# An attention block's softmax maxima: folded by ScalarE's shift, turned as four blocks one step later

## The chip, the cores and the metric

The kernel runs on one core of one Trainium2 chip. The metric is the device time of one execution in microseconds (us); the time before is 3637.75 us, the median of three runs (3636.31 to 3641.64). The engines are called PE (TensorE's matmuls; PEld its weight loads), ACT (ScalarE), DVE (VectorE), POOL (GpSimd) and SP (the engine that issues most DMAs). PE writes to the accumulation memory PSUM, of which this kernel uses all eight banks in the attention stage; ACT and DVE read it.

## What is computed

The reference is one block of a transformer with modulated layer norms, on x of shape 8 x 1024 x 256: attention with 16 heads of 64, then a mixture of 8 experts of which each takes its 512 best tokens. All of it is float32. Cut to what matters here:

```
h = layernorm(x) * (1 + ca) + sa
proj = einsum('bpv,havn->bhapn', h, w_qkv)         # q, k, v of 16 heads, N = 64
scores = einsum('bhqn,bhkn->bhqk', q, k) / 8
attn = softmax(scores, axis=-1)                    # needs each query's maximum over 1024 keys
out = einsum('bhqk,bhkn->bhqn', attn, v)
x = x + ga * (concat of out @ w_o)
h = layernorm(x) * (1 + cb) + sb                   # then the router, and the experts
```

The change touches the softmax's maxima, the order of the attention loop, and the places where rows of tokens are turned into columns.

## The kernel before

**Units and steps.** Attention is cut into NSU = 128 units: a batch b, a pair p of heads (j = 0, 1), and a half h of the queries (512 of them, QB). Keys lie on the partitions: key tile c (0 to 7) of a unit gives scores `s` of 128 keys x (2 heads x 512 queries). The loop `while g < 4 * NSU + LAG or steps` (L702) goes through steps g; `u, gm = divmod(g, 4)`, so a unit's scores take four steps (gm = 0 to 3 below "step 0" to "step 3"), two key tiles each. The exponentials of key tile c are taken five steps after its scores, the products with the values six steps after (LAG = 6).

**The order is written out by hand** (`tc.manual_schedule()`, L692): each engine runs its instructions in the order in which the program issues them, and an instruction waits for the data and buffers that it needs. Tasks that don't belong to one unit are hung on steps with `at(g, where, f, ...)` and run by `run(g, where)` in the places "load", "m1", "post", "pool" and "m2" of a step.

**A step before**, in order: "load"; in step 1 `max_spread` of the unit before (L705); the subtractions of the maxima from two older key tiles (`subtract`, L415, DVE; in step 3 the second of them comes after the scores); scores of two new key tiles (`scores_mm` L356 on PE, then `scores_out`: ACT copies them to `p`, L365, and DVE updates the running maximum `top`, L370); "m1" (projections); "post"; the exponentials (`exp_of`, L418, ACT); the values of two older tiles (`values_mm`, L427, PE), after the last of a unit `values_out` (copy `oT`, L436, ACT); `add_up` (L438 to L446, POOL: sums of the exponentials); in step 3 `max_turn` and `split_max`; "pool"; "m2".

**The maxima.** After eight key tiles `top` (128 x 2 x 512) holds for each query the maximum over 8 keys, for 128 key positions. `max_turn` (L372) turns it on PE as eight 128x128 blocks into `tt`; `split_max` (L381) reduces `tt` along the free axis on DVE, negated, and splits each maximum into three bfloat16 parts in four small operations. `max_rows` (L395, step 0 of the next unit, "m1") turns the parts to rows `pn`, which ACT copies to `nr` (L404). `max_spread` (L407) multiplies them with ones, which leaves the negated maximum of every query on all partitions in `less`. `subtract` adds `less` to the kept scores.

**Buffers in PSUM.** `ps_s` has two buffers of two banks for the scores (tag "s"), which `tt` uses too. `ps_b` has one (two banks) for `less`, `ps_av` one bank for `av`, and `ps_m` one bank, tag "mm". This single `mm` buffer is taken in turn by the projections `pq` (L321) and `pv` (L338), `pn` (L399), `pd` (L462), the output projection `po` (L537), the turned rows `ptx` (L295) and `pth` (L574) and the router's product `pl` (L589). The next user waits until the last one has been read.

**Other tasks of the attention loop.** `qk_task` and `v_task` project queries, keys and values of the coming pair: three projections a unit, one in each of steps 1, 2 and 3. `den_out` (L451, step 0, "m2") sums the exponentials over the keys into `pd`; ACT copies it to `den` (L470), and `den_load`, `den_inv`, `den_spread`, `den_mul` bring the reciprocals back through DRAM and scale `oT`, which is stored to DRAM. `ln_task` normalises 256 rows of a coming batch and turns them (`ln_out`, L286). `out_proj`, `out_norm`, `out_turn`, `out_route`, `out_exp`, `out_score`, `out_store` finish the batch before: output projection, residual, second norm, router. `free_slot` gives `ln_out`, `out_proj` and `out_turn` a step 3 ("behind" the turn of the maxima), and `out_route` a step 1 or 2.

Turns of rows, before, are products with the identity over two halves of 64 columns:

```
for m in range(2):
    c0 = k * P + m * N
    nc.tensor.matmul(pt[m * N : (m + 1) * N, k, i * P : (i + 1) * P],
                     xt[:, i, c0 : c0 + N], ident, start=True, stop=True)
```

Of the kernel before, what the change touches and what calls it, by code (L numbers as in the profile page):

```python
# [37 lines left out]
P = 128  # L38
# [4 lines left out]
def adaln_block(  # L43
# [178 lines left out]
    def mod_rows(i):  # L222
# [13 lines left out]
        for i in (0, 3):  # L236
# [3 lines left out]
            size = small.tile([B, D], F32, tag="at", name=f"size{i}", bufs=2)  # L240
# [45 lines left out]
    def ln_out(b, t):  # L286
        if t == 0:
            hTs[b] = work.tile([P, KC, S], F32, tag="hT", name=f"hT{b}")
        xt = ln_x.pop((b, t))[0]
        pt = ps_m.tile([P, KC, 2 * P], F32, tag="mm", name=f"ptx{b}_{t}")  # L290
        for k in range(KC):
            for i in range(2):
                for m in range(2):
                    c0 = k * P + m * N
                    nc.tensor.matmul(  # L295
                        pt[m * N : (m + 1) * N, k, i * P : (i + 1) * P],
                        xt[:, i, c0 : c0 + N], ident, start=True, stop=True,
                    )
        for k in range(KC):
            nc.vector.tensor_scalar(  # L300
                hTs[b][:, k, 2 * t * P : (2 * t + 2) * P], pt[:, k, :],
                modT[:, KC + k, b : b + 1], modT[:, k, b : b + 1],
                op0=ALU.mult, op1=ALU.add,
            )
# [66 lines left out]

    def max_turn(u):  # L372
        top = tops.pop(u)
        turned[u] = ps_s.tile([P, 8, P], F32, tag="s", name=f"tt{u}")
        for j in range(2):
            for t in range(4):
                nc.tensor.transpose(  # L377
                    turned[u][:, 4 * j + t, :], top[:, j, t * P : (t + 1) * P], ident
                )

    def split_max(u):  # L381

        tt = turned.pop(u)
        nm = tt[:, :2, :8]
        nc.vector.tensor_reduce(nm[:, 0, :], tt, AX.X, ALU.max, negate=True)  # L385
        part = [
            parts_of[u % 2][:, :, :, i].rearrange("p t j -> p j t") for i in range(3)
        ]
        whole, rest = (nm[:, i, :].rearrange("p (j t) -> p j t", j=2) for i in range(2))
# [5 lines left out]
    def max_rows(u):  # L395
# [7 lines left out]
        rows_of[u] = work.tile([P, QB], BF16, tag="nr", name=f"nr{u}")  # L403
# [139 lines left out]
    def out_add(b, t, po):  # L543
        n = f"{b}_{t}"
        x1 = o_x[b, t]
        tmp = small.tile([P, D], F32, tag="at", name=f"at{n}", bufs=2)
# [18 lines left out]
    def out_turn(pool, b, t, tag="mm"):  # L565
# [3 lines left out]
        for i in range(2):  # L569
            h2 = o_h[b, t + i]  # L570
            for k in range(KC):
                for m in range(2):
                    c0 = k * P + m * N
                    nc.tensor.matmul(  # L574
                        pt[m * N : (m + 1) * N, i, k, :], h2[:, c0 : c0 + N], ident,
                        start=True, stop=True,
                    )
# [60 lines left out]
    taken = set()  # L638

    def free_slot(g, behind=False):  # L640
        while g in taken or g % 4 == 0 or behind != (g % 4 == 3):
            g += 1
        taken.add(g)
        return g

    for t in range(NT // 2):
        at(-15 + t, "m2", ln_out, 0, t)
        ln_task(1, t, free_slot(39 + 4 * t, True))
    for b in range(B):
        for p in range(NP):  # L650
            P0 = 8 * (b * NP + p)
            for i, g in enumerate((-7, -6, -5, -2)):
                at(P0 + g, "m1", qk_task, b, p, i)
            if p % 2 == 0:
                for t, g in enumerate((-9, -3, -1, 5)):
# [4 lines left out]
            at(P0 + 17, "load", den_load, b, p)  # L660
            at(P0 + 18, "post", den_inv, b, p)
            at(P0 + 19, "load", den_spread, b, p)
            at(P0 + 20, "pool", den_mul, b, p)
        if b + 1 < B:
            if b + 2 < B:
                for t in range(NT // 2):
                    ln_task(b + 2, t, free_slot(64 * (b + 1) + 39 + 4 * t, True))
            for t in range(NT):
                g = free_slot(64 * (b + 1) + 19 + 4 * t, True)
# [3 lines left out]
                if t % 2:  # L673
                    g = free_slot(g + 2, True)
                    at(g, "m2", out_turn, ps_m, b, t - 1)
                    g = free_slot(g + 1)
                    at(g, "m2", out_route, ps_m, b, t - 1)
                    at(g + 1, "post", out_exp, b, t - 1)
                    at(g + 2, "post", out_score, b, t - 1)
                    at(g + 3, "pool", out_store, b, t - 1)  # L680
    for u in range(NSU):
        at(4 * u + 4, "m1", max_rows, u)
        if u < NSU - 1:
            at(4 * u + 12, "m2", den_out, u)
# [6 lines left out]

    with tc.manual_schedule():  # L692
# [9 lines left out]
        while g < 4 * NSU + LAG or steps:  # L702
            u, gm = divmod(g, 4)
            run(g, "load")
            if gm == 1 and 0 < u <= NSU:  # L705
                max_spread(u - 1)
            u1, gm1 = divmod(g - LAG + 1, 4)
            late = [(u1, 2 * gm1 + i) for i in range(2) if 0 <= u1 < NSU]

            for uc in late[: 1 if gm == 3 else 2]:  # L710
                subtract(*uc)
            if 0 <= u < NSU:
                for c in (2 * gm, 2 * gm + 1):
                    scores_out(u, c, scores_mm(u, c))
            if gm == 3 and late:
                subtract(*late[1])
            run(g, "m1")
            run(g, "post")
            for uc in late:
                exp_of(*uc)  # L720
            u1, gm1 = divmod(g - LAG, 4)
            if 0 <= u1 < NSU:
                for c in (2 * gm1, 2 * gm1 + 1):
                    values_mm(u1, c)
                    if u1 == NSU - 1:
                        if c == 0:
# [354 lines left out]
```

## Time and profile before

| | |
|---|---|
| median of 3 runs | 3637.75 us |
| the profiled execution | 3636.69 us, span 3635.0 us |
| granted PE clock over the span | 0.983 |
| attention loop, first to last `less` product | 82.3 to 3214.8 us |
| PE busy in it | 3095.78 of 3132.50 us |
| DVE, ACT, POOL busy in it | 2674.07, 2354.09, 2533.91 us |
| after the loop: last output projections, search, experts | some 420 us |

Profiles are of one execution. A row of the timeline gives the start, the length, the engine, the line, the operation, what it writes and reads with their shapes, how many instructions were merged into it, and in brackets how long the engine was idle before it and what ended that. PE's ends are modelled, so PE work is best read from start to start. Busy time is summed for each engine; the last rows of some of the costliest groups around the change:

```
L356 PE MATMUL s<-qk,qk 64*128 64x512 f32 x4096 | 1024.9, 612 | 36.1 <-DVE parts L393 32.3
L370 DVE TENSOR_TENSOR top<-top,s 128x1024 f32<-128x1024 f32 x768 | 936.9, 1220 | 259.9 <-ACT p L365 218.2
L385 DVE TENSOR_REDUCE tt<-tt 128x8 f32<-128x1024 f32 x128 | 157.4, 1230 | 67.7 <-PE tt L377 67.6
L377 PE MATMUL tt<-ident,top 128*128 128x128 f32 x1024 | 139.9, 280 | 3.1 <-DVE top L370 3.1
```

The columns are line, engine, operation, output and inputs, shapes and count; then busy us and mean ns of one; then the idle time of the engine just ahead of them and what ended most of it.

### The profile page before, as it was taken

How to read it: one execution, taken by the hardware profiler on the slowest of the kernel's cores; microseconds unless marked ns; L12 is line 12 of the kernel's file. 1: busy time of each engine (PE TensorE's matmuls, PEld its weight loads, DVE VectorE, ACT ScalarE, POOL GpSimd, SP SyncE). 2: the span in 40 equal slices, each digit the busy share in tenths (PEclk: the TensorE clock that was granted, in tenths of full speed). 3: DMA queues.
4: the chain of work that ended last, by engine and by line, in shares of the span. 5: the costliest groups of instructions: out<-in, count | busy, mean ns of one | idle time of the engine just before them, and what ended most of it. 6: DMA issues, size and time to landing. Idle time of an engine off the chain costs nothing. (4 is left out here: it accounts for less than half of the span.)

```text
span 3635.0 us, 54304 instructions
## 1 busy us (share of the span) xinstructions
PE 3462.8 (95%) x20670; PEld 1460.7 (40%) x20670; DVE 2904.0 (80%) x3651; ACT 2432.8 (67%) x2980; POOL 2657.6 (73%) x1537
## 2 busy tenths in 40 slices
PE   6999999999999999999999999999999999982898
PEld 2333334334433434334433344344334344342565
DVE  4888888888888888888888888888888888857442
ACT  2777777777777777777777777777777777740111
POOL 0778778887788777977788888877888887851232
PEclk9999999999999999999999999999999999995999
DMA  3010011111121122111211112011311112133332
GB/s 76 13 38 29 24 31 57 45 43 41 49 56 38 45 61 55 33 39 45 65 52 30 52 45 62 30 52 43 62 38 43 46 51 56 51 85 122 94 99 41
DMA packets 189653, 185.40 MB, mean 51 GB/s; under 512 B 48952, under 2 KB 167240, under 8 KB 189264
## 3 DMA queue, kind: packets, MB, share of 16 engines
q1 hardware_dynamic: 170736, 160.04, 15.6%
q0 software_dynamic: 7168, 12.72, 1.8%
q10 hardware_dynamic: 11488, 9.18, 0.9%
q8 instruction: 163, 2.67, 0.3%
q14 instruction: 98, 0.80, 0.1%
HBM read 127.06 MB, written 63.21 MB: 52 GB/s over the span
## 5 line engine op out<-in xcount | busy, mean ns | idle before, releaser
L446 POOL TENSOR_TENSOR acc<-acc,p 128x1024 f32<-128x1024 f32 x762 | 1805.2, 2369 | 361.8 <-ACT p L418 328.5
L365 ACT COPY p<-s 128x1024 f32<-128x1024 f32 x1024 | 996.2, 1018 | 421.1 <-PE s L356 414.5
L415 DVE TENSOR_TENSOR p<-p,less 128x1024 f32<-128x1024 f32 x1024 | 1206.7, 1210 | 32.8 <-PE less L412 30.0
L370 DVE TENSOR_TENSOR top<-top,s 128x1024 f32<-128x1024 f32 x768 | 936.9, 1220 | 259.9 <-ACT p L365 218.2
L418 ACT ACTIVATE p<-p 128x1024 f32<-128x1024 f32 x1024 | 1041.7, 1057 | 75.0 <-DVE p L415 74.7
L356 PE MATMUL s<-qk,qk 64*128 64x512 f32 x4096 | 1024.9, 612 | 36.1 <-DVE parts L393 32.3
L427 PE MATMUL av<-p,v 128*64 128x512 f32 x4096 | 968.1, 593 | 1.8 <-ACT oT L436 1.8
L356 PEld LDWEIGHTS s<-qk,qk 64*128 64x128 f32 x4096 | 358.3, 186 | 528.7 <-issue 240.1
L321 PE MATMUL pq<-hT,wq 128*64 128x512 f32 x2048 | 495.9, 605 | 2.7 <-ACT qk L328 1.4
L427 PEld LDWEIGHTS av<-p,v 128*64 128x64 f32 x4096 | 280.6, 137 | 461.9 <-issue 367.3
L443 POOL TENSOR_TENSOR acc<-p,p 128x1024 f32<-128x1024 f32 x127 | 301.6, 2375 | 190.4 <-ACT p L418 190.4
L321 PEld LDWEIGHTS pq<-hT,wq 128*64 128x64 f32 x2048 | 124.1, 136 | 343.0 <-issue 211.4
L338 PE MATMUL pv<-wq,hT 128*64 128x256 f32 x2048 | 251.0, 387 | 2.6 <-ACT qk L326 1.4
L1006 ACT ACTIVATE h<-ph,b_sb 128x512 f32<-128x512 f32 x64 | 44.0, 687 | 274.6 <-PE ph L1002 274.6
L385 DVE TENSOR_REDUCE tt<-tt 128x8 f32<-128x1024 f32 x128 | 157.4, 1230 | 67.7 <-PE tt L377 67.6
L537 PE MATMUL po<-wo,ot 128*64 128x256 f32 x1792 | 205.7, 382 | 0.0
L338 PEld LDWEIGHTS pv<-wq,hT 128*64 128x64 f32 x2048 | 136.4, 137 | 155.5 <-issue 66.2
L370 DVE TENSOR_TENSOR top<-p,s 128x1024 f32<-128x1024 f32 x128 | 155.9, 1218 | 9.8 <-ACT p L365 9.8
L343 ACT COPY v<-pv 128x512 f32<-128x512 f32 x128 | 74.9, 585 | 129.7 <-PE pv L338 129.7
L377 PEld LDWEIGHTS tt<-ident,top 128*128 128x128 f32 x1024 | 109.6, 140 | 107.2 <-DVE top L370 107.2
L508 POOL TENSOR_TENSOR oT<-oT,rb 128x1024 f32<-128x1024 f32 x63 | 149.9, 2380 | 3.3 <-DMA rb<-rden_d 3.3
L537 PEld LDWEIGHTS po<-wo,ot 128*64 128x64 f32 x1792 | 123.5, 137 | 66.2 <-issue 9.4
(166 smaller groups left out, 2429.7 us busy)
## 6 DMA issues: line engine op xcount, KB each, us to landing
rb<-rden_d SPq DMA_DIRECT2D x128, 256.0 KB
oT_d<-oT SPq DMA_DIRECT2D x62, 512.0 KB
ot<-oT_d SPq DMA_DIRECT2D x56, 512.0 KB
rows_d<-row SPq DMA_DIRECT2D x64, 132.0 KB
rows_d<-gb_d SPq DMA_DIRECT2D x8, 1024.0 KB
w<-in_L_ffn_w_dram ACTq DMA_DIRECT2D x8, 1024.0 KB
w<-in_L_ffn_w_dram SPq DMA_DIRECT2D x8, 1024.0 KB
lnx<-in_L_attn_inputs_dram SPq DMA_DIRECT2D x28, 256.0 KB
```

The lines of the kernel that those rows point to most:

```text
L321: nc.tensor.matmul(pq[m * N : (m + 1) * N, :], wq_of(k, a, 2 * p + m), hTs[b][:, k, sl], start=(k == 0), stop=(k == KC - 1),)
L338: nc.tensor.matmul(pv[m * N : (m + 1) * N, i, :], hTs[b][:, k, t0 : t0 + N], wq_of(k, 2, 4 * g, 4), start=(k == 0), stop=(k == KC - 1),)
L356: nc.tensor.matmul(ps[:, j, :], kt[r, c * P : (c + 1) * P], qt[r, h * QB : (h + 1) * QB], start=True, stop=True,)
L365: nc.scalar.copy(probs[u, c], ps)
L370: nc.vector.tensor_tensor(tops[u], probs[u, 0] if c == 1 else tops[u], ps, ALU.max)
L385: nc.vector.tensor_reduce(nm[:, 0, :], tt, AX.X, ALU.max, negate=True)
L415: nc.vector.tensor_tensor(probs[u, c], probs[u, c], less[u], ALU.add)
L418: nc.scalar.activation(probs[u, c], probs[u, c], AF.Exp)
L427: nc.tensor.matmul(avs[u][j * N : (j + 1) * N, :], v[:, c, hh * N : (hh + 1) * N], pT[:, j, :], start=(c == 0), stop=(c == NT - 1),)
L443: nc.gpsimd.tensor_tensor(sums[u], pts[0], pts[1], ALU.add)
L446: nc.gpsimd.tensor_tensor(sums[u], sums[u], pt, ALU.add)
L537: nc.tensor.matmul(po[m * N : (m + 1) * N, :], ot[:, p, m * N : (m + 1) * N], wo[:, p, :], start=(p == 0), stop=(p == NP - 1),)
```

## The change

**The maxima.** A new `max_shift` at the end of step 3 copies, on ACT, each head's opposite half of the partitions of `top` into a tile in the `mm` buffer, moved by 64 partitions: two copies of 64 x 512. A new `max_halves` at the start of step 0 of the next unit takes, on DVE, the maximum of the two halves, head 0 on partitions 0 to 63 and head 1 on 64 to 127: two maxima of 64 x 512. `max_turn` then turns four 128x128 blocks instead of eight, and `split_max` reduces 512 elements a partition instead of 1024.

**The order.** The turn moves from the end of step 3 into step 0 of the next unit, behind that unit's first scores and the older values, which run ahead of it there. `max_rows` moves from "m1" of step 0 to the end of step 0. `max_spread` stays in step 1 but comes after the new scores, and in step 1 both subtractions come after `max_spread`. `den_out` moves one step, to step 1. Projections stand in steps 0, 2 and 3.

**Turns of rows** in `ln_out` and `out_turn` become PE transposes of whole 128x128 blocks; `ln_out`'s scaled copy to `hT` moves from DVE to ACT. `ln_task` now works on the next batch, in its first units, instead of the one after; output projections, `ln_out` and `out_turn` stand in step 2, `out_route` in a new place "m3" of step 1.

In the diff `turning` is `gm == 0 and 0 < u <= NSU`, `late` and `new` are the key tiles to be subtracted and scored in the step, and `values()` issues the products with the values of the two older ones. The diff (the buffer counts of `size`, `nr` and `at`, and that of the last tile's sum, are left out):

```diff
@@ ln_out
-                for m in range(2):
-                    c0 = k * P + m * N
-                    nc.tensor.matmul(
-                        pt[m * N : (m + 1) * N, k, i * P : (i + 1) * P],
-                        xt[:, i, c0 : c0 + N], ident, start=True, stop=True,
-                    )
+                nc.tensor.transpose(
+                    pt[:, k, i * P : (i + 1) * P], xt[:, i, k * P : (k + 1) * P], ident
+                )
         for k in range(KC):
-            nc.vector.tensor_scalar(
-                hTs[b][:, k, 2 * t * P : (2 * t + 2) * P], pt[:, k, :],
-                modT[:, KC + k, b : b + 1], modT[:, k, b : b + 1],
-                op0=ALU.mult, op1=ALU.add,
+            nc.scalar.activation(
+                hTs[b][:, k, 2 * t * P : (2 * t + 2) * P], pt[:, k, :], AF.Identity,
+                bias=modT[:, k, b : b + 1], scale=modT[:, KC + k, b : b + 1],
             )
@@
+    shifted = {}
+    def max_shift(u):
+        shifted[u] = ps_m.tile([P, QB], F32, tag="mm", name=f"shift{u}")
+        for j in range(2):
+            nc.scalar.copy(
+                shifted[u][j * N : (j + 1) * N, :], tops[u][(1 - j) * N : (2 - j) * N, j, :]
+            )
+    def max_halves(u):
+        top, other = tops.pop(u), shifted.pop(u)
+        tops[u] = work.tile([P, QB], F32, tag="half", name=f"half{u}", bufs=1)
+        for j in range(2):
+            r = slice(j * N, (j + 1) * N)
+            nc.vector.tensor_tensor(tops[u][r, :], top[r, j, :], other[r, :], ALU.max)
     def max_turn(u):
         top = tops.pop(u)
-        turned[u] = ps_s.tile([P, 8, P], F32, tag="s", name=f"tt{u}")
-        for j in range(2):
-            for t in range(4):
-                nc.tensor.transpose(
-                    turned[u][:, 4 * j + t, :], top[:, j, t * P : (t + 1) * P], ident
-                )
+        turned[u] = ps_s.tile([P, 2, QB], F32, tag="s", name=f"tt{u}")
+        for t in range(4):
+            sl = slice(t * P, (t + 1) * P)
+            nc.tensor.transpose(turned[u][:, 0, sl], top[:, sl], ident)
     def split_max(u):
-        nm = tt[:, :2, :8]
-        nc.vector.tensor_reduce(nm[:, 0, :], tt, AX.X, ALU.max, negate=True)
+        nm = tt[:, 1, :16].rearrange("p (i t j) -> p i t j", i=2, j=2)
+        nc.vector.tensor_reduce(
+            whole, tt[:, 0, :].rearrange("p (t j k) -> p t j k", t=4, j=2), AX.X, ALU.max,
+            negate=True,
+        )
@@ out_turn
-                for m in range(2):
-                    c0 = k * P + m * N
-                    nc.tensor.matmul(
-                        pt[m * N : (m + 1) * N, i, k, :], h2[:, c0 : c0 + N], ident,
-                        start=True, stop=True,
-                    )
+                nc.tensor.transpose(pt[:, i, k, :], h2[:, k * P : (k + 1) * P], ident)
@@ the tasks' steps
-            for i, g in enumerate((-7, -6, -5, -2)):
+            for i, g in enumerate((-8, -6, -5, -2)):
                 at(P0 + g, "m1", qk_task, b, p, i)
-                for t, g in enumerate((-9, -3, -1, 5)):
+                for t, g in enumerate((-9, -4, -1, 4)):
                     at(P0 + g, "m1", v_task, b, p // 2, t)
-            at(P0 + 17, "load", den_load, b, p)
+            at(P0 + 18, "load", den_load, b, p)
...
-                    ln_task(b + 2, t, free_slot(64 * (b + 1) + 39 + 4 * t, True))
+                ln_task(b + 1, t, 64 * b + 2 + 4 * t)
-                g = free_slot(64 * (b + 1) + 19 + 4 * t, True)
+                g = 64 * (b + 1) + 18 + 4 * (t + t // 2)
                 at(g - 2, "load", out_load, b, t)
                 at(g, "m2", out_proj, ps_m, b, t)
                 at(g + 1, "pool", out_norm, b, t)
...
+                    at(g + 4, "m2", out_turn, ps_m, b, t - 1)
+                    at(g + 7, "m3", out_route, ps_m, b, t - 1)
+                    at(g + 8, "post", out_exp, b, t - 1)
+                    at(g + 9, "post", out_score, b, t - 1)
+                    at(g + 10, "pool", out_store, b, t - 1)
     for u in range(NSU):
-        at(4 * u + 4, "m1", max_rows, u)
         if u < NSU - 1:
-            at(4 * u + 12, "m2", den_out, u)
+            at(4 * u + 13, "m2", den_out, u)
@@ the step
             run(g, "load")
-            if gm == 1 and 0 < u <= NSU:
-                max_spread(u - 1)
-            for uc in late[: 1 if gm == 3 else 2]:
+            early = (1, 0, 2, 1)[gm]
+            for uc in late[:early]:
                 subtract(*uc)
-            if 0 <= u < NSU:
-                for c in (2 * gm, 2 * gm + 1):
-                    scores_out(u, c, scores_mm(u, c))
-            if gm == 3 and late:
-                subtract(*late[1])
+            if turning:
+                max_halves(u - 1)
+            for uc in new:
+                scores_out(*uc, scores_mm(*uc))
+            if gm == 1 and 0 < u <= NSU:
+                max_spread(u - 1)
+            if turning:
+                values()
+                max_turn(u - 1)
+                split_max(u - 1)
+            for uc in late[early:]:
+                if gm != 3:
+                    subtract(*uc)
             run(g, "m1")
             run(g, "post")
-            for uc in late:
+            for uc in late[: 1 if gm == 3 else 2]:
                 exp_of(*uc)
+            if gm == 3:
+                if new:
+                    max_shift(u)
+                for uc in late[early:]:
+                    subtract(*uc)
+                    exp_of(*uc)
+            if not turning:
+                values()
...
-            if gm == 3 and 0 <= u < NSU:
-                max_turn(u)
-                split_max(u)
             run(g, "pool")
             run(g, "m2")
+            run(g, "m3")
+            if turning:
+                max_rows(u - 1)
```

## The prediction

> **What bounds the kernel now.** First the page's engine shares and its clock row.
>
> ```profile
> PE 3462.8 (95%) x20670; PEld 1460.7 (40%) x20670; DVE 2904.0 (80%) x3651; ACT 2432.8 (67%) x2980; POOL 2657.6 (73%) x1537
> PEclk9999999999999999999999999999999999995999
> ```
>
> Then the totals of the attention stretch alone, from the first `less` product (82.3 us) to the last (3214.8 us): 127 units in 3132.5 us, 24.67 us a unit, PE busy 3095.8 us of it. Idle PE is worth 37 us in all, so PE work sets the time. Then the timeline of one unit, in which PE rows follow each other without gaps:
>
> ```profile
> 1504.53 1.95 PE L338 MATMUL pv<-wq,hT 128*64 128x256 f32 x16
> ...
> 1506.31 1.89 PE L427 MATMUL av<-p,v 128*64 128x512 f32 x8
> 1506.52 0.59 ACT L343 COPY v<-pv 128x512 f32<-128x512 f32 x1 [0.74 <-PE pv L338]
> ...
> 1507.00 2.00 ACT L418 ACTIVATE p<-p 128x1024 f32<-128x1024 f32 x2
> ...
> 1508.12 1.99 PE L356 MATMUL s<-qk,qk 64*128 64x512 f32 x8
> ...
> 1508.91 0.57 ACT L436 COPY oT<-av 128x512 f32<-128x512 f32 x1
> ...
> 1519.14 1.09 PE L377 MATMUL tt<-ident,top 128*128 128x128 f32 x8
> ...
> 1520.16 1.09 PE L295 MATMUL ptx<-ident,lnx 128*64 128x128 f32 x16
> ```
>
> From start to start: pv to av 1.78 us, av to s 1.81, s to the next row (pq at 1510.04) 1.92, eight turns 1.02, ptx 1.02. A second thing to see: a projection that ends on PE is copied out by ACT 1.99 us after it started (1504.53 to 1506.52), and rows of one engine in a chain overlap by about 0.1 us (1506.52 + 0.59 against 1507.00).
>
> Last, waits that show what the single buffers do:
>
> ```profile
> 42.38 1.94 PE L321 MATMUL pq<-hT,wq 128*64 128x512 f32 x8 [0.69 <-ACT qk L328]
> ...
> 3219.28 1.15 PE L427 MATMUL av<-p,v 128*64 128x512 f32 x4 [1.80 <-ACT oT L436]
> ```
>
> and from the list of waits (us in total, times, longest):
>
> ```profile
> DVE top L370 <- ACT p L365: 228.0, 238, 2.4
> ```
>
> A projection can't start before the last user of the one `mm` buffer has been copied out; `av` can't before `oT` has; and the running maximum of a key tile waits for ACT's copy of the same scores.
>
> **The change, part by part** (steps 0 to 3 of a unit; c0 to c7 are its key tiles; PE sums are start to start).
>
> Saved on PE: four turns instead of eight. Half of 1.02 is 0.51; with a change of array shape on top (scores cost 1.92 after another shape, 1.81 after `less`, so 0.11) 0.62; I take 0.55, 0.47 saved in 128 units: 60 us. The turns of `ptx` and `pth` on the whole array are four such turns in place of 1.02 us: 0.47 x 56 in the stretch = 26 us. Idle PE at the turn: up to 37 us. One more change of shape (turns, then a projection): -0.11 x 127 = -14 us. Together 109 us: this is what PE work alone promises.
>
> Added off PE: two shifts of 64x512 on ACT. No such row; the nearest are 0.57 (`oT`, 512 columns) and 1.01 (scores, 1024). I take 0.58 each, bounds 0.4 and 1.0. Two maxima of 64x512 on DVE: between 0.43 (L547, 256 columns) and 1.22 (1024), 0.69 each; the reduction halves from 1.23 to 0.70. DVE's total grows by 128 x (1.38 - 0.53) less 30 us of `hT`, about 80 us on 2674; ACT's by 128 x 1.1 and the `hT` writes on 2354. Neither reaches PE. The `hT` writes on ACT come last in step 2, behind its exponentials, and the next scores are copied later; I cost them at nothing, and without that cover at 28 x 1 us.
>
> Moved: this decides. In step 1 the diff puts the scores c2, c3 ahead of `max_spread`, and both subtractions (c0, c1 of the unit before) behind the maxima of c2, c3 on DVE. `den_out` moves from step 0 to step 1. No projection is left in step 1; there is one each in steps 0, 2 and 3. Each engine runs its queue in order, so I follow one unit from the start of its step-0 projection on PE:
>
> - ACT copies that projection out at +1.99 (row: 0.58, then 2.00 for the two exponentials queued behind it, then 0.59 for `nr`, which `max_rows` now issues last in step 0). With 0.1 overlaps, `nr` ends at +4.98.
> - Behind `nr` on ACT stands the copy of c2, start +4.88, 1.01 long. DVE's maximum of c2 waits for it. The maxima of c2, c3 take 2.54 (row pair), the two subtractions 2.35 with 0.08 overlap: the second ends at +10.75.
> - ACT's exponential of c1 waits for that: 1.06, then `oT` 0.57, then `den` 0.37 (the copy of `pd`), 0.2 of overlap: +12.58, and 0.1 until PE sees it.
> - `pd` holds the one `mm` buffer. The step-2 projection waits for it on PE, and everything behind it.
>
> That is 12.66 us from the step-0 projection to the step-2 projection. PE's own work between them is projection 1.78, `pn` 0.25, scores 1.92, `less` 0.23, values 1.82, `pd` 0.57, scores 1.92: 8.49. So PE stands 4.2 us: about 0.9 ahead of `pn` (its buffer waits for the projection's copy), 0.3 ahead of `less` (for `nr`), 3.0 ahead of the step-2 projection. From there to the next step-0 projection PE runs through: 1.78 + 1.82 + 1.92 + 1.78 + 1.82 + 1.92 + 1.82 + 0.55 = 13.4. **A unit takes 26.1 us before extra work, the stall included.** The shift isn't on this loop: from the last maximum over two shifts, an exponential, two score copies, c1's maximum, reduction, four small splits and a subtraction I reach the last exponential within 0.1 us of when ACT is free. At 1.0 us a shift it would add 0.8 a unit, 100 us.
>
> Extra work on top, all in PE's running part: 56 output projections of 3.60 (L537 row of 32, start to start) = 202; 56 turns of 0.55 = 31. The 28 router products now stand behind `pd` in step 1 and take its wait, so the next scores (1.92) and they (0.52) come after it: 2.45 x 28 = 69. The 28 score normalisations (L611 to L615, 1.9 us on DVE) now stand between the maximum and the last subtraction in step 3 and use up 0.9 us of cover ahead of the turns: 1.0 x 28 = 28. Stretch: 127 x 26.1 + 202 + 31 + 69 + 28 = 3645, against 3132.5: +512. On the profiled execution (3636.7, its span 3635.0, 1 us under the median of 3637.75): 4148.
>
> What the stall does to the clock is the other term. The trace has one lone stall of that kind:
>
> ```profile
> 3213.40:3216.80 3.40, 3.40 (x24) 0.90 (x22) 2.44 (x3) 2.46 (x4) 3.32 (x2) 1.00 0.00 0
> 3216.80:3220.20 3.40, 1.60 (x22) 0.69 (x18) 3.37 (x6) 3.33 (x6) 3.32 (x2) 0.99 0.03 4
> 3220.20:3223.60 3.40, 3.40 (x18) 0.70 (x20) 3.33 (x9) 3.33 (x4) 0.48 (x3) 0.51 0.06 16
> ...
> 62.90:66.30 3.40, 2.00 (x10) 0.59 (x10) 2.90 (x4) 1.56 (x3) 0.00 (x0) 1.00 0.06 10
> 66.30:69.70 3.40, 3.40 (x18) 1.07 (x16) 1.22 (x1) 2.07 (x4) 0.00 (x0) 1.00 0.00 0
> ```
>
> The columns are the stretch, its length, busy PE, PEld, DVE, ACT and POOL, then the granted clock. After 3.4 us with PE busy 1.60 the clock was 0.51 for the next 3.4; after 2.00 busy it stayed. A 3.0 us hole leaves under 1.6 busy in some 3.4 us piece for about nine positions in ten. A half-clock piece costs 1.7 us where it falls on work; some falls on the rest of the hole. I take 1.4 us a unit (bounds 0 and 1.7), on PE's running part: 127 x 1.4 = 178. **4148 + 178 = 4326, and I predict 4325.**
>
> The Trainium skill, TensorE: Matmul & The Clock Gate, section "What's actually happening", asks for a wholly idle window of about 3.4 us before the clock halves. By that rule a 3.0 us hole costs nothing more and the time would be 4148; the row, with a window half busy, speaks against it, and the row decides.
>
> Moved without a price: normalisation of the next batch into steps early in the current one (its `mm` buffer is free after the projection's copy); the denominators' DMAs on SP one step later as a chain, `den` waiting for its copy, with a step (6 us) and more to the next issue; the first output load only three steps behind the store it reads, about 18 us for 512 KB; POOL's sums, 4.8 us a step of over 6. If the load came late, a few us in seven batches.
>
> **The rivals.**
> 1. PE work alone counts: DVE and ACT keep up, and the step-2 projection finds its buffer free. 3637 - 109 = **3528**. For it: PE is 95% busy, the saved rows are real. Against it: the queue orders above. The point from which it decides: subtractions that end less than 5 us after ACT's copy of c2. 10%.
> 2. The loop as above at full clock: **4148**. For it: the rule of the clock isn't known from one event. 22%.
> 3. The maximum's own chain is the longer loop (shift near 1.0, or handing over partitions slower than a copy) with half clock: **4430** and more. The two shifts have no row. 8%.
> 4. Stall and savings cancel: needs a stall of 0.9 us a unit, which no order of these rows gives. 2%.
>
> **Numbers.** The forecast has 58%, own range 4250 to 4430. With rival 2 it makes 80%: 4080 to 4450. Below about 0.2% this kernel's times can't be told apart. Faster 0.10, the same 0.02, slower 0.88.
>
> **What would show it.** Right: PE idle ahead of a projection (L321) released by ACT `den` L470, near 3 us, in nearly every unit; `less` products about 26 us apart where no output projection lies between; subtraction rows of c0, c1 behind two maxima; PEclk tenths below 9 all along. Turns: four rows of L377's kind, near 0.55 a unit. Wrong: PE rows without gaps at step 2, or a granted clock of 1.00 beside 3 us holes (then 4148).

## The result, and the profile after

The changed kernel takes 4445.6 us (median of four runs, 4443.4 to 4449.3) against 3639.7 for the kernel before beside it: **1.222 times** as long, interval 1.220 to 1.224. That is 808 us more than the time the prediction started from, and inside its range at the upper edge (4450). The profiled execution has a span of 4447.5 us.

The page of the changed kernel, its engine shares and its clock row:

```profile
PE 3715.4 (84%) x19390; PEld 1467.5 (33%) x19390; DVE 3018.3 (68%) x3843; ACT 2607.0 (59%) x3300; POOL 2654.7 (60%) x1537
PEclk9999999899998999989999899989999899897699
```

PE was busy 95% of the span; now 84%, of a longer span, although it has 1280 instructions fewer. Its busy time has grown by 253 us with less work in it: the same products took longer, because the granted clock (mean 0.919, 0.983 before) fell again and again. No other engine has taken over: DVE, ACT and POOL all show lower shares than before. When all shares fall, look at waits.

The list of waits of the changed kernel (us in total, times, longest):

```profile
PE pq L317 <- ACT den L483: 273.5, 96, 3.0
PE pl L597 <- ACT den L483: 129.2, 28, 4.8
PE av L440 <- ACT p L431: 64.7, 24, 3.0
```

Before, this list began on PE with 41.7 us at a line of the search after the loop. Now the first row is the step-2 projection, which stands 2.85 us in 96 units until the denominators have been copied out of the `mm` buffer; in the 28 units with a router product that product stands there, 4.6 us each. The third row is another hole, in step 0 of 24 units.

The timeline of one ordinary unit, from the step-0 projection to the step-2 projection:

```profile
292.45 1.95 PE L334 MATMUL pv<-wq,hT 128*64 128x256 f32 x16
294.45 0.58 ACT L339 COPY v<-pv 128x512 f32<-128x512 f32 x1 [2.41 <-PE pv L334]
294.93 2.06 ACT L431 ACTIVATE p<-p 128x1024 f32<-128x1024 f32 x2
296.89 0.57 ACT L417 COPY nr<-pn 128x512 bf16<-128x512 bf16 x1
297.36 1.93 ACT L361 COPY p<-s 128x1024 f32<-128x1024 f32 x2
298.41 2.54 DVE L366 TENSOR_TENSOR top<-top,s 128x1024 f32<-128x1024 f32 x2 [2.51 <-ACT p L361]
...
300.87 4.61 DVE L428 TENSOR_TENSOR p<-p,less 128x1024 f32<-128x1024 f32 x4
302.12 2.19 ACT L431 ACTIVATE p<-p 128x1024 f32<-128x1024 f32 x2 [2.83 <-DVE p L428]
304.21 0.57 ACT L449 COPY oT<-av 128x512 f32<-128x512 f32 x1
304.68 0.38 ACT L483 COPY den<-pd 128x256 f32<-128x256 f32 x1
305.11 3.39 PE L317 MATMUL pq<-hT,wq 128*64 128x512 f32 x8 [2.85 <-ACT den L483]
```

Read it downwards: behind the projection's copy and two exponentials stands `nr`; `nr` holds back the copies of the new scores on ACT, the first of them holds back two maxima on DVE, behind these stand the subtractions, behind the first two of these an exponential, behind it `oT` and `den`, and only then PE goes on. Each row starts where the one before it lets go. The last row has a second message: eight products that took 1.94 us in the profile before take 3.39.

Why, the windows of the same unit show (stretch, length, busy PE, PEld, DVE, ACT and POOL, then the granted clock, the DMA share and GB/s):

```profile
302.70:305.60 2.90, 0.49 (x2) 0.20 (x4) 2.78 (x3) 2.83 (x5) 1.79 (x2) 0.97 0.45 178
305.60:309.00 3.40, 3.40 (x11) 0.98 (x8) 2.90 (x3) 1.74 (x3) 1.15 (x1) 0.52 0.02 6
309.00:312.40 3.40, 3.40 (x18) 1.07 (x16) 0.68 (x1) 2.81 (x4) 2.18 (x1) 1.00 0.00 0
```

PE busy 0.49 of 2.90 us, then 3.4 us at 0.52 of the clock with PE busy throughout, then the full clock. Over the loop the records hold 121 pieces at half the clock, of 3.4 or 6.8 us each, 594 us in all; the loop before has none.

The new operations themselves, in the list of groups:

```profile
L384 DVE TENSOR_TENSOR half<-top,shift 64x512 f32<-64x512 f32 x256 | 174.6, 682 | 3.0 <-ACT shift L374 1.3
L374 ACT COPY shift<-top 64x512 f32<-64x512 f32 x256 | 149.6, 584 | 42.9 <-DVE rd L619 19.2
L399 DVE TENSOR_REDUCE tt<-tt 128x8 f32<-128x512 f32 x128 | 88.8, 694 | 1.5 <-PE tt L391 0.8
```

Each shift takes 584 ns, each half maximum 682 ns, the reduction 694 ns (1230 before). None is waited for to speak of.

From one `less` product to the next a unit with neither a projection of the output nor a router product takes mostly 26.7 to 29.7 us, in the main 27.5 to 28.4 (24.67 was the mean over all units before). A unit with a projection, a router product and a score normalisation takes 38.7 to 40.9.

### The profile page after: what moved, and what is told of

Read it like the earlier page. It is cut to its first block, busy times and chain, and to the rows that moved or that the text cites. A ratio compares the mean times of both kernels' runs of the same rounds, so it can differ in the third digit from the quotient of the medians.

```text
span 4447.5 us, 52421 instructions
## 1 busy us (share of the span) xinstructions
PE 3715.4 (84%) x19390; PEld 1467.5 (33%) x19390; DVE 3018.3 (68%) x3843; ACT 2607.0 (59%) x3300; POOL 2654.7 (60%) x1537
## 5 line engine op out<-in xcount | busy, mean ns | idle before, releaser
L431 ACT ACTIVATE p<-p 128x1024 f32<-128x1024 f32 x1024 | 1061.0, 1055 | 450.6 <-DVE p L428 438.1
L440 PE MATMUL av<-p,v 128*64 128x512 f32 x4096 | 1043.1, 630 | 70.7 <-ACT p L431 64.7
L352 PE MATMUL s<-qk,qk 64*128 64x512 f32 x4096 | 1067.2, 640 | 6.9 <-DVE top L366 6.9
L317 PE MATMUL pq<-hT,wq 128*64 128x512 f32 x2048 | 630.6, 747 | 276.5 <-ACT den L483 273.5
L317 PEld LDWEIGHTS pq<-hT,wq 128*64 128x64 f32 x2048 | 147.5, 162 | 663.8 <-ACT den L483 352.9
L334 PE MATMUL pv<-wq,hT 128*64 128x256 f32 x2048 | 261.0, 399 | 2.7 <-ACT qk L322 1.4
L324 ACT COPY qk<-pq 128x512 f32<-128x512 f32 x128 | 74.9, 585 | 271.4 <-PE pq L317 271.4
L560 DVE TENSOR_TENSOR at<-po,mod 128x256 f32<-128x256 f32 x56 | 23.8, 425 | 275.5 <-PE po L550 275.5
L384 DVE TENSOR_TENSOR half<-top,shift 64x512 f32<-64x512 f32 x256 | 174.6, 682 | 3.0 <-ACT shift L374 1.3
L374 ACT COPY shift<-top 64x512 f32<-64x512 f32 x256 | 149.6, 584 | 42.9 <-DVE rd L619 19.2
```

The source lines that it names most:

```text
L317: nc.tensor.matmul(pq[m * N : (m + 1) * N, :], wq_of(k, a, 2 * p + m), hTs[b][:, k, sl], start=(k == 0), stop=(k == KC - 1),)
L334: nc.tensor.matmul(pv[m * N : (m + 1) * N, i, :], hTs[b][:, k, t0 : t0 + N], wq_of(k, 2, 4 * g, 4), start=(k == 0), stop=(k == KC - 1),)
L352: nc.tensor.matmul(ps[:, j, :], kt[r, c * P : (c + 1) * P], qt[r, h * QB : (h + 1) * QB], start=True, stop=True,)
L384: nc.vector.tensor_tensor(tops[u][r, :], top[r, j, :], other[r, :], ALU.max)
L431: nc.scalar.activation(probs[u, c], probs[u, c], AF.Exp)
L440: nc.tensor.matmul(avs[u][j * N : (j + 1) * N, :], v[:, c, hh * N : (hh + 1) * N], pT[:, j, :], start=(c == 0), stop=(c == NT - 1),)
```

## The experiments

The theory was the prediction's: a loop of ACT and DVE through the single `mm` buffer, with a half clock after each hole. Against it stood that the clock costs nothing, that the fold itself is the cost, and, after the result, the question where the last 120 us were (4325 forecast, 4445.6 measured).

**The hole filled (e1_fill).** In 96 units PE does two key tiles' score products twice, inside the hole, so that it isn't idle there.

```diff
@@ scores_mm
-        for j in range(2):
+        for j in (0, 1, 0, 1) if c in (4, 5) and u % 16 not in (0, 7, 10, 13) else (0, 1):
```

> The changed kernel with PE work added: in 96 of the 128 units the products for the scores of c4 and c5 are done twice into the same buffers, ahead of ACT's copies, so that about 1.9 us of PE's 3.0 us wait for the den copy is filled. Theory (the wait itself is set by ACT and DVE, and it halves PE's clock behind it): the loop gets no longer, the half-clock pieces vanish in these units, 96 x 1.4 to 1.7 us fewer: 4280 to 4310. Rival (the low clock costs nothing, the time is the queue loop's alone): 4440 to 4450. Rival (PE work sets the time): 96 x 1.9 more, some 4630.

Measured 4301.3, 1.1824 [1.1806, 1.1842]. More work on PE saved 144 us. From its list of waits, and its span with the granted clock:

```profile
PE pq L317 <- ACT den L483: 115.8, 96, 2.8
```

```profile
core 0: 4299.4 us, clock 0.956
```

The hole shrinks by most of the added work, and the loop gets no longer: ordinary units are 26.1 us, the prediction's own figure without half clock, and the half-clock time falls from 594 to 249 us. 144 us of time for 345 us of half clock is 0.42 us for each: an estimate from this one pair of runs, and the price used below.

**The denominators' copies first (e2_den_first).** In step 1 ACT's `oT` and `den` go ahead of the exponentials; by its loop condition the products of the last unit's key tiles 4 and 5 with the values, and their sums, are left out.

```diff
@@ the loop, ahead of the exponentials of step 1
+            if gm == 1:
+                values()
+                if old:
+                    values_out(u2)
+                run(g, "m2")
...
-            if not turning:
+            if gm > 1:
                 values()
-            if old and gm2 == 3:
-                values_out(u2)
```

> The changed kernel with one thing moved: in step 1 ACT's copies of oT and den are issued ahead of the two exponentials instead of behind them; PE's order stays. Theory (the step-2 projection waits for the den copy behind exponentials, subtractions and maxima): PE's wait ahead of L317 for den goes from 3.0 to under 0.3 us, the next limit is scores waiting for the running maximum in step 3, about 24.5 us a unit; time 3900 to 4050. Rival (the chain of the maximum through the shift sets the unit): above 4380.

Measured 3991.9, 1.0973 [1.0956, 1.0990]. One order on one queue is worth 454 us. The wait of `pq` for `den` is gone from the list; what comes next is scores that wait for maxima, and values that wait for exponentials, 24.5 us a unit.

**The score normalisation a step later (e3_score).**

```diff
-                    at(g + 9, "post", out_score, b, t - 1)
-                    at(g + 10, "pool", out_store, b, t - 1)
+                    at(g + 10, "post", out_score, b, t - 1)
+                    at(g + 11, "pool", out_store, b, t - 1)
```

> The changed kernel with the router's score normalisation on DVE one step later (step 0 instead of step 3) and its store with it. Theory (in units that have both an output projection and a normalisation, the last subtraction and exponential come 3 us late for the values of step 0, and the clock halves once more): about 24 units lose 5 to 6.5 us less, 4290 to 4325. Rival (those units are long because the router's product waits for pd): change under 30 us.

Measured 4360.5, 1.1986 [1.1967, 1.2004]: 85 us less, where 120 or more was expected. The normalisation does cost much more than the forecast's 1.0 us (those units fall from some 40.6 to 36.0 us, and the wait of `av` is gone from the list), but the router's hole (129.4 us) is as it was.

**POOL's sums left out (e11_pool_quiet).** In the long units DVE's two scalings of 128x8, which should be short, were long. Rows of the changed kernel's timeline, one such unit, DVE and POOL:

```profile
2234.07 2.35 POOL L459 TENSOR_TENSOR acc<-acc,p 128x1024 f32<-128x1024 f32 x1
2235.20 1.50 DVE L561 TENSOR_TENSOR ox<-ox,at 128x256 f32<-128x256 f32 x1
...
2241.22 2.35 POOL L459 TENSOR_TENSOR acc<-acc,p 128x1024 f32<-128x1024 f32 x1
2241.26 2.47 DVE L623 TENSOR_SCALAR row<-ex,rd 128x8 f32<-128x8 f32 x2
2243.64 2.34 DVE L428 TENSOR_TENSOR p<-p,less 128x1024 f32<-128x1024 f32 x2
2244.89 1.06 ACT L431 ACTIVATE p<-p 128x1024 f32<-128x1024 f32 x1 [2.65 <-DVE p L428]
2245.99 1.08 PE L440 MATMUL av<-p,v 128*64 128x512 f32 x4 [2.85 <-ACT p L431]
```

Add start and length: POOL's first addition ends at 2236.42, DVE's residual addition at 2236.70; POOL's second at 2243.57, DVE's scalings at 2243.73. DVE ends just behind POOL both times. So it is throughout this trace: all 45 residual additions that take over 1 us end 0.28 us after a POOL addition, all 22 such scalings 0.03 us after one. Before the change the scalings were long as well, the residual addition was not:

```profile
L548 DVE TENSOR_TENSOR ox<-ox,at 128x256 f32<-128x256 f32 x56 | 23.8, 426 | 1.9
L615 DVE TENSOR_SCALAR row<-ex,rd 128x8 f32<-128x8 f32 x64 | 52.1, 857 | 1.1
```

Down the last rows of the unit the delay reaches the subtraction, the exponential and PE. So:

```diff
@@ add_up
-        else:
-            for pt in pts:
-                nc.gpsimd.tensor_tensor(sums[u], sums[u], pt, ALU.add)
```

> Left out: POOL's running additions of the exponentials (six of 2.35 us a unit; only the first addition of two key tiles stays), so the denominators are those of two key tiles of eight. Everything else stays as in the changed kernel. If DVE's residual addition (56 times, mean 1.16 us, single rows up to 2.34) and the two scalings of the score normalisation (mean 0.96 us, up to 2.34) are long because POOL's addition runs beside them, they fall to the 0.4 and 0.22 us of their short rows; the last subtraction of a unit with a normalisation then ends some 2 us earlier, its values wait under 1 us instead of 3.0, and 25 units lose that hole and one half-clock piece: 4330 to 4400. If they are long for a reason of their own (their tiles, their shapes), the means stay and the time stays within 20 us of 4446.

Measured 4323.0, 1.1881 [1.1861, 1.1901]: 123 us less. The two groups by shape, first of the changed kernel, then of this one:

```profile
L561 DVE TENSOR_TENSOR ox<-ox,at 128x256 f32<-128x256 f32 x56 | 64.9, 1159 | 1.9
L623 DVE TENSOR_SCALAR row<-ex,rd 128x8 f32<-128x8 f32 x64 | 58.9, 964 | 1.1
```

```profile
L558 DVE TENSOR_TENSOR ox<-ox,at 128x256 f32<-128x256 f32 x56 | 23.8, 425 | 1.9
L620 DVE TENSOR_SCALAR row<-ex,rd 128x8 f32<-128x8 f32 x64 | 12.6, 243 | 1.1
```

1159 falls to 425 ns and 964 to 243 (lines are three lower). The long units come down from some 40 us to 34.2 to 35.8, beside 34.55 as the prediction's terms add up (26.1 + 1.4 + 3.6 + 2.45 + 1.0); `PE pq L317 <- ACT den` is still there with its 273.7 us. With the hole in the values gone as well, most of the missing 120 us is found.

**The router's hole filled too (e5_fill_all).** As e1_fill, and in the router's units PE does the denominators' products seven times.

```diff
@@ den_out
-        den_mm(pd, sums.pop(u))
+        for _ in range(7 if (u + 3) % 16 in (0, 7, 10, 13) else 1):
+            den_mm(pd, sums[u])
+        sums.pop(u)
```

> e1_fill with the other holes filled as well: in the units with a router's product the products for pd are done seven times instead of once, which keeps PE busy for 3.4 of the 4.8 us that it waits there. Theory (the half-clock pieces come from these holes, and the 249 us of them left in e1_fill go): the loop at full clock, 26.1 us a unit, with the 3 us stall of the units with projection and normalisation left: 4150 to 4210. Rival (half the clock has another cause, or the router's waits are a longer loop): above 4270.

Measured 4277.8, 1.1761 [1.1741, 1.1780]: a miss, just beyond the line drawn for the rival. The list of waits says why:

```profile
PE av L440 <- ACT p L431: 65.2, 25, 3.0
PE pl L599 <- ACT den L485: 59.3, 28, 2.2
```

Half of the router's hole is left, the values' hole is whole, and with them 167 us of half clock. Filling treats the clock where it fills, and nothing else.

**The order without the fold (e7_order_8).** The changed kernel's order, with eight blocks turned and no shift or half maximum.

```diff
@@ max_turn
+        for j in range(2):
+            for t in range(4):
+                nc.tensor.transpose(
+                    turned[u][:, 4 * j + t, :], top[:, j, t * P : (t + 1) * P], ident
+                )
@@ the loop
-            if turning:
-                max_halves(u - 1)
...
-                if new:
-                    max_shift(u)
```

> The changed kernel with its order but without the fold: top is turned as eight blocks and reduced over 1024, no shift and no halves. Theory (the queue loop from the step-0 projection to the den copy sets the unit, the fold is off it): PE's four more turns, 0.45 us a unit, come on top: 4480 to 4530. Rival (shift and halves are on the chain that sets the unit): faster than the changed kernel, under 4400.

Measured 4521.9, 1.2432 [1.2412, 1.2453]. Without the fold it is 76 us slower still, and `PE pq L317 <- ACT den` reads 273.5 us, 96 times, as before the edit: taking the fold away doesn't shorten the loop. The number fell into the expected range for another reason than the one given, though. A wait that stood at 12.9 us in 14 units before the edit is now in nearly every unit:

```profile
PE pn L413 <- DVE parts L407: 188.4, 120, 3.4
```

Eight turns and the longer reduction come ahead of the parts, PE waits for these, and `nr` comes later; against that stand some 423 us of half clock instead of 594. So the 76 us are not the price of four turns.

**The fold without the order (e6_fold_old).** The kernel before, its eight turns replaced by shift, half maxima and four turns in the old place, the end of step 3.

```diff
@@ max_turn
+        max_shift(u)
+        max_halves(u)
...
+        for t in range(4):
+            sl = slice(t * P, (t + 1) * P)
+            nc.tensor.transpose(turned[u][:, 0, sl], top[:, sl], ident)
```

> The kernel before with the other part alone: maxima folded by two shifts and two half maxima, turned as four blocks, all in the old place at the end of step 3. Theory (there the fold is a longer chain in front of a PE that has nothing else to do: exponential, two shifts 1.2, two halves 1.3, less 0.5 of turns and 0.5 of reduction, 2.6 to 3.0 us a unit, and the clock halves behind some of these holes): 3970 to 4190. Rival (the fold saves what it saves on PE): under 3640.

Measured 4316.7, 1.1866 [1.1846, 1.1885]: worse than the worst that was expected. Its longest wait, from 300 to 3900 us:

```profile
PE tt L397 <- DVE half L388: 515.1, 120, 6.3
```

PE waits 4.3 us at each turn for shift and half maxima, and pays 594 us of half clock on top. So the fold does need the turn moved behind other work; the two parts of the change can't be added up, as each costs some 680 to 890 us alone.

**The turns of rows alone (e4_old_turns).** The kernel before, with whole-array transposes for `ptx` and `pth`.

```diff
-                for m in range(2):
-                    c0 = k * P + m * N
-                    nc.tensor.matmul(
...
+                nc.tensor.transpose(
+                    pt[:, k, i * P : (i + 1) * P], xt[:, i, k * P : (k + 1) * P], ident
+                )
```

> The kernel before with one part of the change alone: rows of tokens are turned as whole 128x128 blocks (ptx and pth), nothing else. Theory (these turns stand in the hole behind the turn of the maxima, where PE waits for the split anyway): the same, within 0.2% of before, 3632 to 3645. Rival (as the sum of saved PE work had it): 56 x 0.47 = 26 us less, about 3612.

Measured 3634.7 over 11 runs, 0.9990 [0.9981, 0.9999]: 3 us where the rows promise 26. In the kernel before PE waits 32.3 us ahead of scores for the maxima's parts, 71 times, and the turns of rows stand in front of that wait. Here the same wait reads:

```profile
PE s L353 <- DVE parts L390: 64.5, 71, 1.3
```

Within the loop PE is busy 33 us less (3062.9 us, 3095.8 before) and waits 32 us longer there: what the turns leave is waited out.

**The order mended (e8_reorder, e9_late_add, e10_step0).** The fold, the four turns and the later place are kept. In e8 `max_spread` and the first subtraction come ahead of the maxima of c2, c3 on DVE; ACT takes `oT` and `den` ahead of the second exponential of step 1, and `nr` ahead of the second of step 0; the step-0 projection goes ahead of the turns and the values; the score normalisation is one step later. Of its diff the core:

```diff
+            for i, uc in enumerate(new):
+                ps = scores_mm(*uc)
+                if gm == 1 and i == 0 and u > 0:
+                    max_spread(u - 1)
+                    for lc in late[:1]:
+                        subtract(*lc)
+                scores_out(*uc, ps)
+                if gm == 2 and i == 0:
+                    held_exp()
...
+            elif gm == 1:
...
+                for uc in late[:1]:
+                    exp_of(*uc)
+                held.extend(late[1:])
+                values()
+                if old:
+                    values_out(u2)
```

> The fold kept, the order mended at every wait that the traces show: in step 1 less comes between the two scores, one subtraction ahead of the maxima and one behind, ACT copies oT and den ahead of the exponential of c1, which goes behind the copy of c4; in step 0 the projection comes ahead of the turns and the values, and nr ahead of the last exponential; the router's normalisation in step 0. Theory (the time was lost to the order of the queues, not to the fold): 22.6 to 23.3 us a unit without extra work, 3640 to 3750. Rival (the fold itself costs more than it saves in any order): above 3900.

Measured 3844.6, 1.0569 [1.0551, 1.0587], beyond the expected 3750, though the loop fell: ordinary units are 23.2 us, units with an output projection 28.0. There the step-0 projection waits for the half maxima (98.0 us in 61 units for `pq`, 84.7 in 42 for `pv`), which stand on DVE behind the long residual additions. e9 takes that addition and the second norm's statistics to step 0 and the normalisation of scores to step 2:

```diff
-                at(g + 1, "pool", out_norm, b, t)
+                at(g + 2, "post", out_add2, b, t)
+                at(g + 3, "pool", out_norm, b, t)
...
-                    at(g + 10, "post", out_score, b, t - 1)
-                    at(g + 11, "pool", out_store, b, t - 1)
+                    at(g + 12, "post", out_score, b, t - 1)
+                    at(g + 13, "pool", out_store, b, t - 1)
```

> e8_reorder with two pieces of VectorE work moved: of the output projection only the first product (which frees the mm buffer) stays in step 2, the residual's sum and the norm's statistics go to step 0; the router's normalisation goes to step 2. Theory (in units with a projection these 2.1 us, 1.5 of them a wait of DVE beside POOL, hold up the last maxima, then shift and halves, and the step-0 projection waits for their buffer): units with a projection go from 28.0 to about 26.3 us, half-clock pieces vanish: 3690 to 3750. Rival (the projection's own buffer wait makes them long): over 3810.

Measured 3748.2, 1.0304 [1.0286, 1.0321]. The wait that is left:

```profile
PE pq L317 <- DVE half L384: 65.7, 61, 2.3
```

e10 puts work ahead of that wait: PE's step 0 becomes values, the four turns, the projection, values, and the last exponential goes behind the new scores' copies on ACT.

```diff
             if turning:
-                run(g, "m1")
+                values(slice(0, 1))
                 max_turn(u - 1)
-                values()
+                run(g, "m1")
+                values(slice(1, 2))
                 split_max(u - 1)
...
-                        exp_of(*uc)
+                        held.append(uc)
```

> e9_late_add with step 0 in another order: on PE the values of c4, the four turns, the projection, the values of c5; on ACT the exponential of c5 behind the copies of the two new scores. Theory (the 0.8 us hole left in every unit is PE waiting for the halves, and there is work to put into it): 22.0 to 22.6 us a unit without extra work, 3590 to 3660, level with the kernel before or a little under it. Rival (DVE, busy nearly all the time, is the bound by now): no better than e9_late_add within 20 us.

Measured 3619.4 (3617.7 to 3619.8), **0.9948 [0.9932, 0.9965]**: 0.5% faster than the kernel before. PE's rows of step 0, and its page:

```profile
275.23 1.08 PE L440 MATMUL av<-p,v 128*64 128x512 f32 x4
276.24 0.66 PE L391 MATMUL tt<-ident,half 128*128 128x128 f32 x4
276.82 1.94 PE L317 MATMUL pq<-hT,wq 128*64 128x512 f32 x8
278.59 1.03 PE L440 MATMUL av<-p,v 128*64 128x512 f32 x4
```

```profile
PE 3424.0 (95%) x19390; PEld 1386.6 (38%) x19390; DVE 2954.8 (82%) x3843; ACT 2578.1 (71%) x3300; POOL 2665.2 (74%) x1537
```

PE is back at 95%, no half clock in the loop, ordinary units 22.5 us. The turns take 0.58 from start to start. Of the 109 us that PE's work alone promised, some 19 are had: PE's busy time is 39 us below the kernel before, and the gain is in the units with neither an output projection nor router work (22.5 to 23.1 us in the mean, 23.6 before). Units with a projection take 25.8 to 27.2, where they took 25.7 to 26.2; which waits keep them there wasn't followed further.

## Why the prediction was right, point by point

**The number: inside the stated range, by 4 us and with luck.** The forecast was 4325 with an own range of 4250 to 4430, and 4445.6 lies above that; it lies inside 4080 to 4450, which was widened to take in rival 2. What was right is the mechanism.

**The loop: right, step for step.** Every link that it named is a row of the timeline above, in that order. From the step-0 to the step-2 projection it forecast 12.66 us; the unit shown takes 12.66, the median of the 96 units is 12.85. The hole ahead of the step-2 projection was forecast at 3.0 and is 2.85; the one ahead of `pn` at 0.9 and is 0.7. The unit of 26.1 us stands free of the clock in e1_fill. e2_den_first shows the loop as cause by breaking it at one link, e7_order_8 that the loop stays without the fold.

**The unit costs: right.** Shift 0.58 taken, 0.584 measured; halves 0.69 and 0.682; reduction 0.70 and 0.694; four turns 0.55 and 0.59.

**The half clock: right in mechanism, and nearly in size because two errors offset each other.** It took nine positions of a hole in ten to be followed by half clock; its own condition (under 1.6 us busy of 3.4) gives some eight in ten for a hole of 3.0 us, and 71 of the 96 holes ahead of `pq` were followed. It priced the router's holes like the others; of the 27 of 4.8 us, 22 were followed by 6.8 us of half clock. Without POOL's sums there are 468 us of it, at 0.42 some 196 us; 178 was taken. In the changed kernel itself it is 594 us, some 250; most of the surplus belongs to the next point. The Trainium skill, TensorE: Matmul & The Clock Gate, section "What's actually happening", names an idle window of about 3.4 us as what takes PE to half its clock, and the prediction read that as wholly idle. Read so, the trace doesn't agree: holes of 2.85 us, with PE busy 0.49 us in the stretch around one, were followed by 3.4 us at 0.52. The measurement decides, as the prediction had it.

**What was mis-sized: the score normalisation, "1.0 x 28 = 28".** It was priced by the 1.9 us that the group took on DVE in its old place, of which 0.9 were taken as covered. The 1.9 nearly held: its scalings were long in the old place already (857 ns, 964 after). The cover did not. In the same units the residual addition, 0.43 us before, now stands beside a POOL addition and takes 1.16 us in the mean; behind it and the scalings the last subtraction, the exponential and the values came late enough for a second hole of 2.7 us (64.7 / 24), and that brought a second half-clock piece, which the term left out. The 21 units with a projection, a router product and a normalisation last 40.06 us in the mean, where the terms add up to 34.55. That is 116 us, nearly all of the 123 by which the loop (3946 us) is longer than forecast (3645 + 178).

What the normalisation's place costs by itself, e3_score measures: some 85 us in place of 28 (in its new place it costs next to nothing: units with a projection last 31.3 us with it and 31.2 without). In e3_score these 21 units still last 35.97 us, where the terms without the normalisation give 33.55: some 51 us more, in which the 6.8 us of half clock after each router's hole and the longer residual addition have a part; how they divide wasn't measured. e11_pool_quiet, which takes POOL's sums away and leaves every instruction of PE, ACT and DVE, saves 123 us, but not all of that is this term: some 20 of it fall in the 35 units with a projection and neither router product nor normalisation (31.11 to 30.55 us in the mean).

**The rivals.** PE work alone (3528) fell with the first row of the waits. The loop at full clock (4148) fell with the clock row: the price of the half clock taken off, 4445.6 - 250, leaves some 4195. The maximum's own chain (4430 and more) has nearly the right number and the wrong reason: shifts are 584 ns, and PE waits only 12.3 us in all for the half maxima. Stall and savings don't cancel in this order; in e10_step0's order the savings win by 0.5%.

**The savings were too high as a term of the first rival.** e4_old_turns is worth 3 us of the 26 taken for the rows' turns, as PE's wait for the parts grew by what they saved. That had no weight here, as PE wasn't the bound after the change, but it would have had in a forecast of 3528.

## What to carry to other kernels

Where engines run in a fixed order through single buffers, follow one unit from the release of a buffer to its next use, engine by engine, before adding up what an engine saves: here two copies behind two exponentials were worth 454 us, and all the saved rows, once the order let them count, 19. Price a hole on PE with the clock that follows it, and a small DVE operation by what POOL does beside it in the new place, not by its mean in the old one. A fold that lengthens a chain needs other work put ahead of the place that waits for it, on the engine that waits; here only then did it pay.

## What the hardware showed that was not expected

**DVE behind POOL.** A DVE addition of 128x256 (0.43 us alone) and a scaling of 128x8 (0.24) lasted until POOL's running addition of 128x1024 ended, up to 2.3 us, and were short again when that addition was left out. The Trainium skill, SBUF — State Buffer, section "Who interferes with whom", describes a pair of ports that DVE and GpSimd share and that one of them holds for an instruction; the rows agree. The half maxima, which read one input from PSUM, took 682 ns beside POOL's sums and without them.

**A clock that halves after holes of less than 3 us.** In the changed kernel it did so after 71 of the 96 holes of 2.85 us, mostly for 3.4 us, and after all 27 of the router's holes of 4.8 us, in 22 of them for 6.8 us. Which holes, the trace's clock records show. All half-clock pieces start on one raster of 3.413 us (138.19, 192.81, 220.12 and 247.42 us are 16, 8 and 8 of these apart). Two neighbouring windows on it, around the hole shown above:

```profile
302.04:305.45 3.41, 0.56 (x4) 0.20 (x4) 3.41 (x4) 3.26 (x5) 2.30 (x2) 1.00 0.38 150
305.45:308.86 3.41, 3.41 (x10) 0.98 (x8) 2.79 (x4) 1.75 (x3) 1.30 (x1) 0.50 0.02 7
```

With the loop cut along this raster, PE was by these records (its ends are modelled) busy at most 1.44 us in the 122 windows at full clock after which the clock fell, and at least 1.44 us in the 859 after which it stayed. In e1_fill the two values are 1.46 and 1.54; in e7_order_8 they overlap, from 1.43 to 1.53. So it counts how much of a hole lies within one window. Doubling PE's products in the hole, work whose result changes nothing, bought 144 us.
